# Cross-attention with LayerNorm on one core: the last 14 tiles' orders dealt anew, residual and row sum merged for eight tiles, and the last step of five tiles shared by three engines

## The chip, the core and the metric

The kernel runs on one core of a Trainium2 chip. The core has a matrix engine (TensorE, PE in the profile), three engines for elementwise work (VectorE or DVE, ScalarE or ACT, GpSimd or POOL), a queue engine (SyncE, SP), and 16 DMA engines that serve the queues. The metric is the device time of one execution in microseconds (us); smaller is better. Times given as medians come from several executions; the profile shows one execution.

## The reference

```python
qs = (q @ wq).reshape(Bq, Lq, H, HD).transpose(0, 2, 1, 3)      # q = x, 4 x 2048 rows of 512
ks_ = (k @ wk).reshape(Bq, Lk, H, HD).transpose(0, 2, 1, 3)     # k = v = context, 4 x 77 rows of 512
vs = (v @ wv).reshape(Bq, Lk, H, HD).transpose(0, 2, 1, 3)
scores = jnp.einsum('bhqd,bhkd->bhqk', qs, ks_) / jnp.sqrt(jnp.float32(HD))
scores = jnp.where(mask[:, None, :, :], -jnp.inf, scores)
attn_w = jax.nn.softmax(scores, axis=-1)
attn = jnp.einsum('bhqk,bhkd->bhqd', attn_w, vs).transpose(0, 2, 1, 3).reshape(Bq, Lq, H * HD)
out = attn @ wo + q
mu = jnp.mean(out, axis=-1, keepdims=True)
var = jnp.mean((out - mu) ** 2, axis=-1, keepdims=True)
return (out - mu) / jnp.sqrt(var + EPS) * gamma + beta
```

16 heads of 32, float32 throughout, 8192 rows of x, a padding mask over the 77 keys.

## The kernel before

The 8192 rows are 64 tiles of 128 rows. Four tiles make a group (queries are projected for a group at a time), two tiles a block (attention is applied to a block at a time). float32 products are made of three passes over high and low parts, so a projection of 128 x 512 is 12 matmuls.

The order of all work is written out by hand: `ORDER` is one long string of words, and each word issues a few instructions. Each engine runs its own instructions in the order of the string and waits, where it must, for data, for a buffer or for one of the eight PSUM banks, which `SLOTS["mm"]` deals out one by one. So a word's place in the string matters only against words of the same engine and queue. A word is a letter with a tile, block or visit number:

| word | engine | what it does (line) |
|---|---|---|
| `Q`, `q` | PE, DVE | project queries (L292), copy them out of PSUM (L306) |
| `S` | PE | scores of a tile, 64 narrow matmuls (L429) |
| `T`, `e` | DVE, ACT | row maxima of four heads (L446), their exponentials with row sums (L461) |
| `r`/`h`, `n`/`m`, `t` | DVE, POOL, DVE | reciprocal sums (L471, L482 by halves), weights times them (L476, L488 by halves), transpose (L497) |
| `P`, `U` | SP, POOL or ACT queue (last letter `s`, `g`, `a`) | one of twelve transfers that regroup a block's or a tile's weights (L508) |
| `V`, `W` | PE | weights times values for a block (L522) or a tile (L537), narrow matmuls |
| `a`/`c`, `b`/`d` | ACT, DVE | high part (L551) and low part (L555) of that product, out of PSUM |
| `O` | PE | output projection of a tile, 12 matmuls (L603) |
| `!`, `^` | PE, ACT | open a bank with one matmul (L577), seed it with x (L580), so that `O` adds to x |
| `+`, `$` | DVE | residual to SBUF (L606) or left in PSUM (L609) |
| `s`, `=` | DVE, ACT | mean and variance by bn_stats (L650, L652), or by a Copy pass and a Square pass with sums (L656, L657) |
| `u`, `@` | POOL | one over the root (L663 to L666), or that and a shift (L670) |
| `y`, `z`, `>` | DVE | centre and times gamma (L679); times the root, plus beta (L682), by halves (L686) |
| `%`, `k` | ACT | scale and shift (L674, L635) |
| <code>&#124;</code>, `f` | POOL | times gamma or plus beta (L642), one pass or both |
| `w`, `<`, `x`, `g` | SP (half a `<` on ACT) | store of a tile (L645) or half (L692), loads |
| `i`, `j`, `v`, `M` | ACT, POOL, POOL, DVE | split x for the next group, root for two earlier tiles, mask |

Up to tile 47 all tiles are finished the same way: `+ s v k f w`. From tile 48 on (`LATE`) each tile has its own mix of the words above. `o_proj` from tile 50 on puts the four matmuls that need the low part last. Before the change, PE's order from S50 to the end is

```
S50 V22 S51 Q54 Q55 O45 O44 S52 V23 S53 Q56 Q58 S54 O46 Q59 S55 Q57 V24 O47 S56 O48 V25 S57 O49 O51
S58 Q61 Q62 Q63 S59 Q60 V26 S60 O50 V27 S61 O53 O52 S62 O54 S63 O55 V28 V29 O57 !63 O56 !58 O59 V30
O58 O61 O60 W62 W63 O62 O63
```

and ACT's order behind its last exponential is `^58 ^63 %50 =56 a30.1 a30.0 =55 U63.0a %54 U63.1a =58 =59 =61 c62 %57 =60 c63 =62 =63 <63.1`.

## Time and profile before

| | |
|---|---|
| median of 3 runs | 506.64 us (506.02 to 507.09) |
| the profiled execution | 507.38 us, span 505.5 us |
| TensorE clock granted | 0.996 |
| busy share | PE 98%, DVE 93%, ACT 94%, POOL 82% |
| share of the last chain on PE | 96% |
| bytes moved | 110.97 MB, 220 GB/s |

The span is the time from the first instruction to the last; the execution's own time is longer by 1.9 us around it. Times in the views are counted from the start of the span. A row of the groups reads: line, engine, operation, output <- input, shapes, count | busy us, mean ns of one | idle time of the engine just ahead of them and what ended it. A row of the timeline reads: start, length, engine, line, operation; a row of the chain: start, length, engine, tile and line.

### The profile page before, as it was taken

To read this page: it belongs to the slowest core of one execution; us is meant where nothing else is said; L and a number is where in the kernel's file an instruction comes from. 1 tells how busy PE (TensorE), PEld (TensorE's weight loads), DVE (VectorE), ACT (ScalarE), POOL (GpSimd) and SP (SyncE) were. 2 spreads that over 40 slices of the span, in tenths; PEclk is the share of its full clock that TensorE was granted. 3 is DMA by queue.
4 is the path that set the end of the run, shared out by engine and by line. 5 is a ranking of instruction groups with operands and counts; after the bars stand their busy time and mean duration, and the time that the engine had idled before them with its cause. 6 is when DMAs were issued, how large, how long until landed. Compare 5 with 4: busy or idle time off the path is not lost.

```text
span 505.5 us, 21829 instructions
## 1 busy us (share of the span) xinstructions
PE 496.0 (98%) x6834; PEld 383.8 (76%) x6834; DVE 468.4 (93%) x2556; ACT 473.1 (94%) x2252; POOL 414.5 (82%) x380
## 2 busy tenths in 40 slices
PE   9999999999999999999999999999999999999994
PEld 7987777777777777777778777777877777777772
DVE  5798999999999999999999999999999999999996
ACT  6698999998999999999999999999999999999973
POOL 3664756989978998988899898889989869888894
PEclk9999999999999999999999999999999999999998
DMA  8947768868987676696777687787778787678656
GB/s 302 398 146 219 190 181 193 251 171 241 250 228 234 201 228 192 207 258 201 223 215 232 196 241 202 222 226 219 212 203 231 208 226 234 180 208 223 161 167 260
DMA packets 59521, 110.97 MB, mean 220 GB/s; under 512 B 9441, under 2 KB 12283, under 8 KB 59410
## 3 DMA queue, kind: packets, MB, share of 16 engines
q1 hardware_dynamic: 56658, 103.99, 70.9%
q0 software_dynamic: 2224, 5.05, 3.5%
q8 instruction: 60, 0.98, 0.9%
q10 hardware_dynamic: 528, 0.52, 0.3%
q14 instruction: 51, 0.42, 0.3%
HBM read 41.79 MB, written 16.78 MB: 116 GB/s over the span
## 4 chain that ended last, share of the span: by engine, by line
PE 96%; POOL 1%; DMA 1%; ACT 1%; DVE 0%; issue 0%; DVEq 0%
PE pq L292 35%; PE po L603 34%; PE pa L522 11%; PE sc L429 11%; PE pq L746 1%; PE pk L315 1%; PE pv L354 1%; DMA first_xtl<-xw 1%; POOL xth L642 1%; PE pv L342 0%; POOL mvt L666 0%; ACT AH L551 0%; PE pa L537 0%; DVE xtl L682 0%; ACT xth L674 0%
## 5 line engine op out<-in xcount | busy, mean ns | idle before, releaser
L461 ACT ACTIVATE pbuf<-pbuf,nm 128x77 f32<-128x77 f32 x1024 | 352.6, 351 | 3.7 <-DVE nm L446 3.7
L461 ACT ACTIVATION_READ_ACCUMULATOR pbuf<-pbuf,nm 128x1 f32 x1024 | 196.4, 192 | 0.0
L446 DVE CUSTOM_DVE_ANT_0 pbuf<-sc,mb 128x77 f32<-128x77 f32 x1024 | 171.2, 234 | 6.9 <-PE sc L429 3.7
L476 POOL TENSOR_TENSOR pbuf<-pbuf,ri 128x1232 f32<-128x1232 f32 x63 | 142.7, 2266 | 30.5 <-DVE ri L471 29.1
L603 PE MATMUL po<-woh,AH 128*128 128x512 f32 x256 | 101.6, 397 | 0.0
L292 PE MATMUL pq<-xth,wqh 128*128 128x512 f32 (+1 forms) x256 | 101.4, 396 | 0.2
L603 PE MATMUL po<-wol,AH 128*128 128x512 f32 x256 | 99.9, 390 | 0.0
L292 PE MATMUL pq<-xtl,wqh 128*128 128x512 f32 (+1 forms) x256 | 98.4, 384 | 0.0
L292 PE MATMUL pq<-xth,wql 128*128 128x512 f32 (+1 forms) x256 | 98.2, 383 | 0.0
L497 DVE STREAM_TRANSPOSE B<-pbuf 128x1280 f32<-128x1280 f32 x64 | 96.2, 1503 | 1.6 <-POOL pbuf L476 0.5
L603 PE MATMUL po<-woh,AL 128*128 128x512 f32 x256 | 93.0, 390 | 0.0
L446 DVE DVE_READ_ACCUMULATOR2_ANT nm<- 128x1 f32 x1024 | 85.6, 84 | 0.0
L275 POOL TENSOR_TENSOR xtl<-xtf,xth 128x1024 fp32r<-128x1024 f32 x28 | 67.2, 2403 | 4.3 <-ACT xth L271 4.3
L642 POOL TENSOR_TENSOR o<-o,bet 128x512 f32<-128x512 f32 x51 | 65.9, 1292 | 3.8
L429 PEld LDWEIGHTS sc<-kct,q 32*64 32x64 f32 x4096 | 51.5, 130 | 22.3 <-issue 11.5
L642 POOL TENSOR_TENSOR o<-o,gam 128x512 f32<-128x512 f32 x51 | 67.0, 1313 | 0.0
L429 PE MATMUL sc<-kct,q 32*64 32x77 f32 x4096 | 60.9, 238 | 0.0
L522 PE MATMUL pa<-PT,vsb 96*32 96x256 f32 x992 | 59.5, 382 | 0.0
L603 PEld LDWEIGHTS po<-woh,AH 128*128 128x128 f32 x256 | 48.0, 188 | 12.7 <-issue 1.2
L292 PEld LDWEIGHTS pq<-xth,wqh 128*128 128x128 f32 x256 | 48.1, 188 | 12.5 <-issue 1.2
L603 PEld LDWEIGHTS po<-woh,AL 128*128 128x128 f32 x256 | 47.9, 188 | 10.6 <-DVE AL L555 0.6
L292 PEld LDWEIGHTS pq<-xth,wql 128*128 128x128 f32 x256 | 48.1, 188 | 9.8
(135 smaller groups left out, 638.5 us busy)
## 6 DMA issues: line engine op xcount, KB each, us to landing
PT<-B SPq DMA_DIRECT2D x351, 128.0 KB
xtf<-xT SPq DMA_DIRECT2D x28, 512.0 KB
o<-x SPq DMA_DIRECT2D x56, 256.0 KB
out<-o SPq DMA_DIRECT2D x56, 256.0 KB
PT<-B POOLq DMA_DIRECT2D x20, 128.0 KB, 4.0
PT<-B SPq DMA_DIRECT2D x17, 64.0 KB
stage_a<-wk SPq DMA_DIRECT2D x4, 256.0 KB
stage_a<-xT SPq DMA_DIRECT2D x2, 512.0 KB
```

The lines of the kernel that those rows point to most:

```text
L275: nc.gpsimd.tensor_tensor(l[:, c : c + 2], fx.pop((g, c)), xh[g][:, c : c + 2].bitcast(F32), ALU.subtract)
L292: nc.tensor.matmul(pq, w[:, c, m * P : (m + 1) * P], r[g][:, c, rs], start=(n == 0), stop=(n == 11))
L315: nc.tensor.matmul(pks[m][:, : NB * NK], w[:, c, m * P : (m + 1) * P], ctx_s[c][i], start=(c == 0 and n == 0), stop=(c == NC_D - 1 and n = ...
L354: nc.tensor.matmul(pv[: rows.stop - rows.start], ctx_s[c][i][:, rows], v[c], start=(n == 0), stop=(n == 11))
L429: mm = nc.tensor.matmul(sc[j][r0 : r0 + SR, g * NK : (g + 1) * NK], qs[q, g, rs.start + r0 : rs.start + r0 + SR], kct[q, g, t // TPB, keys ...
L446: nc.vector.tensor_tensor_reduce(pb[:, h // 2, (h % 2) * NK : (h % 2 + 1) * NK], scs[t][j][:, g * NK : (g + 1) * NK], mb[:, t % TPB, keys_ ...
L461: nc.scalar.activation(pb[:, h // 2, (h % 2) * NK : (h % 2 + 1) * NK], pb[:, h // 2, (h % 2) * NK : (h % 2 + 1) * NK], AF.Exp, bias=nmax[t ...
L476: nc.gpsimd.tensor_tensor(pv, pv, rv.to_broadcast((P, NP, 2, NK)), ALU.mult)
L497: nc.vector.transpose(bt.rearrange("p c q r -> p q c r"), pbuf[t % NPB].rearrange("p q (c r) -> p q c r", c=5),)
L522: nc.tensor.matmul(pas[b, g // 2][HD * j : HD * (j + 1), (g % 2) * BLK : (g % 2 + 1) * BLK], vsb[:, 2 * b // TPB, h % 2, HD * (h // 2) : H ...
L603: nc.tensor.matmul(pos[t], a[:, c, rs], w[:, c, :], start=(first and i == 0), stop=(i == len(terms) - 1))
L642: nc.gpsimd.tensor_tensor(od[t], od[t], (gam, bet)[i], (ALU.mult, ALU.add)[i])
```

## The change

`ORDER` is rewritten from the words around S50 to the end, on all engines and queues, with PSUM banks dealt anew for it; everything ahead stays. New words:

- `{` (`residual_sum`): one VectorE instruction adds the residual in PSUM and gives the row sum; a second, of one column, makes the negative mean. `}` (`squares`): ScalarE's Square pass for the variance. Tiles 48, 52, 53, 56, 57, 58, 60 and 63 take this pair in place of `$ s` or `$ =`.
- `-` (`root_act`): ScalarE's Sqrt on one column, `?` (`inverse`): VectorE's reciprocal of it. Tiles 50, 52, 53, 56, 58, 59, 61, 62 and 63 take these in place of GpSimd's `u`; `;` is the shift of tile 50 on VectorE.
- `_` (`scale_centred`): for tiles 51, 57, 58, 59 and 60 VectorE centres into SBUF (`y`), ScalarE multiplies by the root (`_`), GpSimd adds beta (`|`) where VectorE's `z` did both.

One bank is opened with a matmul (`!62`) instead of two (`!58`, `!63`). The profile before has one ACT_TABLE_LOAD, at the start; the first Sqrt (`-50`) stands behind the last exponential. Tile 63 is now projected ahead of tile 62. Transfers for regrouping: SP 83 (before 89), GpSimd 34 (25), ScalarE 0 (3). The new orders:

```
PE from S50: S50 V22 S51 Q55 Q54 Q57 S52 V23 S53 Q59 O44 O45 S54 Q56 Q58 S55 V24 S56 O47 Q63 Q60 O46
  S57 V25 S58 O49 O48 Q61 S59 Q62 V26 S60 O51 O50 S61 V27 O52 S62 O53 S63 O54 V28 O55 O57 V29 O56 O58
  V30 O59 O60 O61 !62 W63 W62 O63 O62
ACT behind the last exponential: a29.1 }57 %55 -50 }56 }53 a30.1 -53 a30.0 }58 -56 _51 }52 -58 %49 =54
  _57 =59 _58 -52 %50 c63 ^62 c62 -59 }60 =61 _59 -61 }63 _60 -63 =62 -62 <63.1
DVE behind t63: {58 ?50 y53 b30.1 y56 ;50 b30.0 ?53 ?56 $59 y58 ?58 z56 y54 y52 z53 z54 $61 {60 ?52 y59
  d63 z52 ?59 d62 y60 {63 y61 ?61 z61 y63 ?63 >63.0 >63.1 y62 ?62 z62
POOL behind the last `n`: u51 P30.5g U62.6g @55 m63.1 m63.0 |55.0 u57 U63.6g U63.8g U63.9g U63.7g U63.3g
  |51.1 |49.0 u54 |55.1 |57.1 |49.1 |58.1 |50.0 u60 |50.1 |59.1 |60.1
```

The code of the diff, with the last lines of the string:

```diff
@@ -114,32 +114,32 @@
...
-y55 @57 U63.9s z56 O60 U63.4s =59 $61 |54.0 U63.10s y58 w53 z52 =61 u59 z55 |50.1 W62 $60 W63 y59 c62 |54.1 w50 y61
-%57 w56 d62 O62 =60 u58 w54 z59 w46 w55 u61 z58 c63 |57.0 z61 $62 w61 w58 d63 O63 |57.1 =62 w52 y60 u60 w57 y62 w59
-u62 =63 z60 z62 w60 u63 y63 w62 >63.1 >63.0 <63.1 <63.0
...
+y58 =54 |49.0 U62.8s ?58 z56 w51 O61 _57 y54 u54 =59 y52 |55.1 z53 z54 _58 w53 !62 |57.1 W63 $61 -52 %50 {60 W62 |49.1
+w57 c63 w56 ?52 y59 ^62 c62 d63 O63 |58.1 w49 -59 w47 z52 }60 ?59 d62 =61 |50.0 w58 w54 y60 w52 O62 w55 {63 _59 u60
+y61 -61 |50.1 }63 ?61 z61 _60 |59.1 y63 w50 -63 =62 w61 ?63 >63.0 >63.1 |60.1 w59 <63.0 -62 y62 <63.1 ?62 z62 w60 w62
...
+    on_act = {int(word[1:]) for word in ORDER.split() if word[0] == "_"}
...
         nc.scalar.activation(od[t], pos[t], AF.Square, bias=mv[:, 3:4], accum_out=mv[:, 1:2])
+        means[t] = mv[:, 3:4]
         by_act.add(t)
+
+    def residual_sum(t):
+        mv = mvs[t, 1] = tiny.tile([P, 4], F32, tag="mvt", bufs=64 - LATE, name=f"mvt_{t}")
+        mn = tiny.tile([P, 2], F32, tag="mnt", bufs=1, name=f"mnt_{t}") if t == 63 else mv[:, 2:4]
+        means[t] = mn[:, 1:2]
+        nc.vector.tensor_tensor_reduce(pos[t], pos[t], od[t], 1.0, 0.0, ALU.add, ALU.add, accum_out=mn[:, 0:1])
+        nc.vector.tensor_scalar(means[t], mn[:, 0:1], -1.0 / D, None, ALU.mult)
+        by_act.add(t)
+
+    def squares(t):
+        mv = mvs[t, 1]
+        nc.scalar.activation(od[t], pos[t], AF.Square, bias=means[t], accum_out=mv[:, 1:2])
...
+    def root_act(t):
         mv = mvs[t, 1]
-        nc.gpsimd.tensor_scalar(mv[:, 3:4], mv[:, 0:1], mv[:, 2:3], -1.0, ALU.mult, ALU.mult)
+        nc.scalar.activation(
+            mv[:, 2:3], mv[:, 1:2], AF.Sqrt, bias=eps[:, :1], scale=1.0 / D if t in by_act else 1.0
+        )
+
+    def inverse(t):
+        nc.vector.reciprocal(mvs[t, 1][:, 2:3], mvs[t, 1][:, 2:3])
+
+    def shift_one(t, eng=nc.gpsimd):
+        mv = mvs[t, 1]
+        if t in by_act:
+            eng.tensor_scalar(mv[:, 3:4], means[t], mv[:, 2:3], None, ALU.mult)
+        else:
+            eng.tensor_scalar(mv[:, 3:4], mv[:, 0:1], mv[:, 2:3], -1.0, ALU.mult, ALU.mult)
...
     def centre(t):
         o = pos.get(t, od[t])
-        m, op = (3, ALU.add) if t in by_act else (0, ALU.subtract)
-        nc.vector.scalar_tensor_tensor(o, o, mvs[t, 1][:, m : m + 1], gam, op, ALU.mult)
+        if t in on_act:
+            pos.pop(t, None)
+            to = od[t]
+        elif t == 63:
+            to = pos[t] = bank(f"pc_{t}")
+        else:
+            to = o
+        m, op = (means[t], ALU.add) if t in by_act else (mvs[t, 1][:, 0:1], ALU.subtract)
+        nc.vector.scalar_tensor_tensor(to, o, m, gam, op, ALU.mult)
+
+    def scale_centred(t):
+        nc.scalar.activation(od[t], od[t], AF.Copy, scale=mvs[t, 1][:, 2:3])
```

More of the change, by code (lines that the diff above doesn't have):

```diff
@@ L116 @@
 P22.8s f38 k41 P22.5s T49.0 a21.1 Q53 g29 e48.2 T49.2 x47 r47 b21.1 n47 e48.3 b21.0 T49.3 T49.1 O43 e48.0 M52.4 f41
-q53 e49.0 t47 O42 e49.3 q52 P23.7s r48 w38 +43 i28 n48 P23.2s s43 k40 P23.4s S50 +42 e49.2 w41 V22 j28 T50.1 P23.10s
-T50.0 P23.6s e50.1 T50.2 P23.1s S51 s42 x46 a22.0 P23.0s e49.1 T50.3 Q54 v21 P23.3s t48 P23.9s f40 k43 P23.11s T51.0
-P23.8s a22.1 Q55 e50.2 T51.2 P23.5s r49 g30 b22.1 x49 n49 e50.3 b22.0 T51.3 T51.1 O45 e50.0 q55 f43 t49 e51.0 q54
-P24.7s O44 e51.3 r50 w40 +45 n50 P24.4s s45 e51.2 P24.3s P24.9s S52 i29 +44 x63 P24.2g M60.4 P24.11s V23 e51.1 T52.2
@@ L121 @@
-P24.1g P24.5s j29 T52.0 P24.6s e52.2 T52.3 S53 P24.0s t50 x51 e52.3 Q56 P24.8s r51 T52.1 n51 a23.0 T53.0 e52.1 s44 Q58
-q56 a23.1 v22 e52.0 T53.2 b23.0 b23.1 P24.10a t51 S54 k44 e53.0 O46 r52 P25.3g P25.7s T54.1 n52 g31 T53.3 e53.2 P25.6s
-T53.1 w43 T54.0 e53.1 Q59 P25.2s T54.3 f44 x60 T54.2 e53.3 P25.11s t52 P25.5s e54.0 P25.9s S55 M56.4 P25.1s r53 +46
-Q57 n53 e54.1 q59 P25.10s T55.0 P25.0s e54.3 T55.2 P25.8s q58 P25.4g V24 e54.2 q57 t53 a24.0 x56 O47 T55.3 P26.6s
-a24.1 r54 x59 s46 e55.2 n54 x48 P26.1s T55.1 P26.8s k42 b24.1 w44 S56 b24.0 P26.9s k45 f42 t54 P26.11s i31 O48 P26.10s
@@ L126 @@
-e55.3 T56.1 T56.0 x52 j31 x57 e55.0 T56.3 P26.4s V25 $48 w42 P26.2s +47 i30 P26.3s T56.2 P26.0g S57 a25.0 P26.7s s48
-j30 e55.1 O49 b25.0 T57.0 a25.1 T57.1 e56.1 r55 T57.3 n55 b25.1 O51 e56.3 T57.2 $49 e56.0 P26.5g t55 S58 e57.0 s49
-P27.1g P27.7s Q61 P27.4g P27.5s s47 e56.2 u49 P27.9s T58.1 P27.11s u48 y48 e57.3 P27.3g T58.0 v23 Q62 +51 e57.1 y49
-r56 z49 n56 e57.2 T58.2 w49 Q63 x58 q61 P27.6s e58.1 z48 P27.8s P27.2g q62 w48 f45 e58.0 x53 T58.3 x50 P27.0s t56 S59
-P27.10s e58.3 Q60 r57 q63 n57 w45 e58.2 T59.2 T59.3 k46 T59.0 V26 e59.3 q60 f46 t57 e59.0 S60 r58 P28.7s T59.1 n58 O50
@@ L131 @@
-e59.2 P28.10s s51 x54 T60.1 P28.11s a26.0 P28.2s T60.0 a26.1 P28.3s P28.5g T60.3 e59.1 P28.8g P28.4s V27 T60.2 P28.6s
-b26.1 k47 P28.1s r59 b26.0 n59 e60.0 P28.0s S61 t58 P28.9s O53 a27.0 +50 a27.1 t59 e60.2 e60.1 T61.0 P29.1g P29.3s O52
-b27.1 P29.2g P29.0s P29.7g T61.3 P29.4s e60.3 P29.11g T61.1 P29.8s P29.10g T61.2 P29.5s e61.3 @51 S62 P29.9s r60 $52
-x62 b27.0 n60 O54 P29.6s e61.0 T62.0 T62.2 e61.2 T62.3 f47 T62.1 S63 e61.1 t60 O55 %51 r61 T63.1 n61 w47 e62.2 x55 +54
-T63.2 e62.1 T63.3 V28 |51.0 t61 e62.3 V29 |51.1 T63.0 P30.8s a28.0 s52 P30.5s a28.1 P30.10g P30.1s $53 e62.0 P30.6g
@@ L136 @@
-P30.11s b28.1 P30.7g P30.2s b28.0 O57 u52 a29.1 P30.9s r62 s50 a29.0 n62 P30.4s e63.0 s53 P30.0s !63 O56 P30.3s b29.0
-e63.1 b29.1 u53 +57 @50 e63.3 t62 !58 O59 e63.2 y53 U62.11s U62.10g U62.4g U62.7s z53 U62.2g ^58 U62.5s h63.0 h63.1
-$56 m63.1 ^63 U62.1s y52 V30 %50 U62.6s s54 m63.0 =56 U62.8s x61 $55 U62.9s U62.0g O58 t63 a30.1 w51 u56 U62.3s a30.0
-=55 @54 b30.0 U63.11s b30.1 U63.6s U63.3g U63.0a s57 O61 U63.5s |50.0 %54 U63.2s $59 U63.1a U63.7s y56 u55 =58 U63.8s
-y55 @57 U63.9s z56 O60 U63.4s =59 $61 |54.0 U63.10s y58 w53 z52 =61 u59 z55 |50.1 W62 $60 W63 y59 c62 |54.1 w50 y61
@@ L141 @@
-%57 w56 d62 O62 =60 u58 w54 z59 w46 w55 u61 z58 c63 |57.0 z61 $62 w61 w58 d63 O63 |57.1 =62 w52 y60 u60 w57 y62 w59
-u62 =63 z60 z62 w60 u63 y63 w62 >63.1 >63.0 <63.1 <63.0
+q53 e49.0 t47 O42 e49.3 q52 P23.7s r48 w38 +43 i28 n48 P23.2s s43 k40 P23.4s P23.8s M60.4 P23.11s e49.2 w41 P23.6s +42
+S50 P23.9g V22 j28 T50.0 T50.2 e49.1 P23.5s T50.3 P23.10s S51 t48 i29 x49 P23.3g P23.1s Q55 P23.0g a22.1 T50.1 e50.2
+b22.1 r49 T51.2 n49 e50.1 T51.3 Q54 T51.1 a22.0 e50.0 j29 t49 Q57 e50.3 q54 P24.6s T51.0 P24.7g g31 e51.2 M56.4 P24.1s
@@ new lines @@
+P24.0g q55 P24.8s P24.10g b22.0 e51.0 S52 P24.9s r50 q57 n50 g30 V23 T52.3 P24.11s e51.1 T52.0 P24.3s T52.1 f40 e51.3
+S53 t50 P24.4s Q59 a23.1 r51 x46 T53.1 e52.1 T53.3 P24.2g T53.2 P24.5g e52.3 s42 n51 O44 T52.2 a23.0 e53.1 b23.1 b23.0
+v21 e52.2 O45 +44 T53.0 e52.0 t51 e53.2 S54 s44 P25.2s P25.4g P25.3s +45 Q56 P25.6g e53.0 P25.5s r52 q59 n52 P25.9s
+T54.1 e53.3 P25.8s T54.0 w40 T54.3 x60 Q58 i30 P25.0g T54.2 r53 t52 e54.2 n53 q56 e54.3 S55 x57 q58 j30 V24 T55.2 x51
+k43 T55.1 i31 T55.0 S56 t53 e54.0 P25.1g P25.7g O47 j31 a24.0 T56.3 P26.3s e54.1 T56.1 P25.11s T56.2 P25.10s e55.1
@@ new lines @@
+T56.0 P26.0s Q63 f43 T55.3 P26.11s a24.1 s45 x62 e55.3 b24.0 r54 +47 Q60 w43 n54 e56.1 P26.7s s47 P26.9s q63 e55.2
+P26.10s P26.5g P26.1s t54 O46 v22 e55.0 x48 P26.6s q60 x56 e56.2 b24.1 P26.4g x61 P26.2s r55 P26.8g n55 S57 +46 k44
+e56.3 V25 T57.3 T57.2 k42 T57.0 f44 S58 T57.1 e56.0 s46 O49 e57.1 t55 v23 w44 x59 a25.1 r56 P27.0s T58.3 k45 P27.1g
+O48 P27.8s T58.0 a25.0 n56 P27.3s b25.1 e57.2 P27.7s +49 b25.0 P27.9s e57.0 T58.1 x63 Q61 f42 P27.5s s49 e57.3 P27.10s
+T58.2 x50 t56 P27.2s e58.3 x58 P27.11g S59 P27.4s {48 e58.2 w42 Q62 r57 T59.0 n57 q61 k46 T59.1 }48 T59.2 e58.1 f46
@@ new lines @@
+V26 q62 T59.3 x52 e58.0 t57 S60 a26.0 u48 y48 O51 P28.2s e59.3 P27.6g b26.0 w46 P28.7s P28.5g z48 a26.1 @49 P28.10s
+r58 e59.0 b26.1 P28.4s T60.1 O50 n58 P28.9s T60.3 e59.1 w48 T60.2 P28.11s T60.0 P28.6s e59.2 P28.8g t58 P28.3s S61
+P28.0s e60.2 V27 P28.1s +50 x53 r59 T61.0 e60.1 n59 T61.2 O52 T61.3 a27.0 T61.1 e60.0 f45 b27.0 t59 e60.3 S62 P29.10s
+a27.1 r60 O53 T62.3 P29.3g e61.1 P29.7s n60 T62.2 x54 b27.1 P29.6s e61.2 T62.0 P29.4s T62.1 P29.0s S63 P29.9g e61.0
+t60 w45 P29.8g O54 P29.1s P29.2g e61.3 P29.11s T63.3 P29.5s T63.0 e62.1 r61 T63.2 n61 x55 V28 T63.1 k47 $51 e62.3 $54
@@ new lines @@
+f47 O55 t61 a28.1 a28.0 b28.1 P30.2s e62.2 s51 P30.9s P30.3g P30.11s b28.0 O57 e62.0 P30.4g {52 P30.10s P30.1s e63.1
+r62 y51 n62 P30.6s s50 P30.0s V29 e63.3 P30.8s $55 P30.7s u51 t62 e63.2 O56 P30.5g s55 a29.0 U62.2s e63.0 U62.6g
+U62.3s b29.0 @55 U62.5s {57 a29.1 U62.0s h63.1 h63.0 }57 m63.1 {56 U62.7s %55 b29.1 O58 U62.1s m63.0 -50 y57 U62.9s
+{53 U62.10s V30 |55.0 U62.4s }56 t63 U62.11s }53 u57 O59 a30.1 {58 U63.11s -53 U63.6g a30.0 U63.0s ?50 y53 U63.8g }58
+U63.2s U63.9g b30.1 -56 _51 U63.10s U63.7g y56 U63.3g U63.4s }52 ;50 b30.0 O60 |51.1 U63.1s -58 ?53 ?56 $59 %49 U63.5s
@@ L149 @@
         "5071263450231746052371462750136427051320465731206457261340752631402357160423751627405361270453201647"
-        "3520614726531074263510234756012374562710436527014320561734206517264350712654032057104627510423576013"
-        "2745032417230547621347065430712634107531043710573105252364"
+        "3520614726531074263510234756012374562710436527014320561734205176451062734651456072435106274301513046"
+        "25137052462734105723401567304256307470263672076172606271430"
     ),
@@ L260, in xattn_layernorm @@
     od, pos, mvs, rns, vd, ris, parts = {}, {}, {}, {}, {}, {}, {}
-    ends, tmps, xs, by_act = {}, {}, {}, set()
+    ends, tmps, xs, by_act, means = {}, {}, {}, set(), {}
+    on_act = {int(word[1:]) for word in ORDER.split() if word[0] == "_"}
     pe_words = [w for w in ORDER.split() if w[0] in "HBQSVWXO"]
@@ L666, in rsqrt_one @@
         nc.gpsimd.tensor_tensor(mv[:, 2:3], mv[:, 2:3], mhalf[:, :1], ALU.pow)
-    def shift_one(t):
+    def root_act(t):
         mv = mvs[t, 1]
-        nc.gpsimd.tensor_scalar(mv[:, 3:4], mv[:, 0:1], mv[:, 2:3], -1.0, ALU.mult, ALU.mult)
+        nc.scalar.activation(
[9 more added lines that the diff above has]
+            eng.tensor_scalar(mv[:, 3:4], mv[:, 0:1], mv[:, 2:3], -1.0, ALU.mult, ALU.mult)
     def scale_one(t):
@@ L795, in xattn_layernorm @@
         "!": lambda k, part: open_bank(k), "^": lambda k, part: seed(k),
+        "-": lambda k, part: root_act(k), "?": lambda k, part: inverse(k),
+        ";": lambda k, part: shift_one(k, nc.vector),
+        "{": lambda k, part: residual_sum(k), "}": lambda k, part: squares(k),
+        "_": lambda k, part: scale_centred(k),
         "@": lambda k, part: (rsqrt_one(k), shift_one(k)), "%": lambda k, part: scale_one(k),
```

## The prediction

> **What bounds the kernel now.** The page comes first: who is busy, and what the chain that ended last is made of.

> ```profile
> span 505.5 us, 21829 instructions
> PE 496.0 (98%) x6834; PEld 383.8 (76%) x6834; DVE 468.4 (93%) x2556; ACT 473.1 (94%) x2252; POOL 414.5 (82%) x380
> PE 96%; POOL 1%; DMA 1%; ACT 1%; DVE 0%; issue 0%; DVEq 0%
> ```

> PE carries 96% of the chain. Stage by stage, with the columns PE, PEld, DVE, ACT, POOL, clock:

> ```profile
> 460.00:476.00 16.00, 16.00 (x177) 11.56 (x176) 15.55 (x83) 15.78 (x82) 15.59 (x17) 1.00 0.74 201
> 476.00:490.00 14.00, 14.00 (x98) 10.26 (x100) 13.30 (x23) 11.60 (x32) 11.89 (x23) 1.00 0.59 163
> 490.00:505.50 15.50, 7.38 (x80) 5.54 (x72) 10.60 (x17) 6.06 (x15) 9.14 (x15) 0.87 0.64 240
> ```

> PE, DVE and ACT are full until 476, POOL nearly; one that falls behind stops PE. From 490 nobody is full: latency bounds the end. The chain in order of time (start, length) prices PE's work; the last rows here are the chain's end:

> ```profile
> 380.02 0.93 PE sc L429 x54
> 380.95 1.86 PE pa L522 x32
> 382.81 0.88 PE sc L429 x56
> 383.69 5.66 PE pq L292 x24
> 389.36 5.44 PE po L603 x24
> 476.17 0.23 PE po L577
> 489.61 1.05 PE pa L537 x32
> 498.61 0.56 POOL mvt L666
> 499.19 0.75 DVE xtl L682
> 499.94 0.68 DVE po L679
> ```

> The timeline at the end:

> ```profile
> 491.17 1.08 PE L537 MATMUL pa<-PT,vsb 96*32 96x128 f32 x32 [0.55 <-DVE po L609]
> 496.84 1.09 PE L603 MATMUL po<-woh,AL 128*128 128x512 f32 x4
> 497.97 0.60 ACT L656 ACTIVATE xtl<-po 128x512 f32<-128x512 f32 x1 [0.34 <-PE po L603]
> 498.69 0.69 ACT L657 ACTIVATE xtl<-po,mvt 128x512 f32<-128x512 f32 x1
> 499.27 0.19 ACT L657 ACTIVATION_READ_ACCUMULATOR xtl<-po,mvt 128x1 f32 x1
> 499.83 0.55 POOL L666 TENSOR_TENSOR mvt<-mvt,small 128x1 f32<-128x1 f32 x1
> 500.71 0.88 DVE L686 SCALAR_TENSOR_TENSOR xtl<-po,mvt,bet 128x256 f32<-128x256 f32 x2
> 501.97 0.33 SPq L692 DMA_DIRECT2D out<-xtl  x1
> ```

> The last matmul ends at 497.93. Statistics, POOL's root and VectorE's halves take until 501.59; the last store is issued at 501.97, and 3.53 us later the span ends.

> **The change part by part.**

> PE's stream. S50 starts at 380.02, and ahead of it PE's order is unchanged. A score visit costs 0.88, a product V 1.86, a W 1.05, an O or Q 2.72 (5.44/2), and the first full-array visit after narrow ones 5.66 - 5.44 = 0.22 more (0.25 taken, since single visits later take 2.92 to 3.00). Before: 14 x 0.88 + 9 x 1.86 + 2 x 1.05 + 30 x 2.72 + 16 switches x 0.25 + 2 opened banks x 0.23 = 117.2, so 497.2; the remainder to 497.93 is the pipe's 0.2 and the 0.5 that W63 waits. After: 14 switches and one opened bank, 116.5. **Gain 0.7.**

> W63's wait. The profile names VectorE, but W63 reads tile 63's regrouped weights, whose transfers are issued behind its transpose. What each engine does there:

> ```profile
> 476.85 0.58 ACT L580 COPY po<-xth 128x512 f32<-128x512 f32 x1
> 479.16 2.54 POOL L488 TENSOR_TENSOR pbuf<-pbuf,ri 128x616 f32<-128x616 f32 x2
> 481.73 1.51 DVE L497 STREAM_TRANSPOSE B<-pbuf 128x1280 f32<-128x1280 f32 x1 [0.53 <-POOL pbuf L488]
> 482.67 6.43 SPq L508 DMA_DIRECT2D PT<-B  x10
> 481.05 1.08 ACT L551 CAST AH<-pa 128x512 fp32r<-128x512 f32 x2 [0.36 <-PE pa L522]
> L674 ACT ACTIVATE o<-o,mvt 128x512 f32<-128x512 f32 x3 | 2.4, 813 | 0.8 <-POOL mvt L670 0.8
> L657 ACT ACTIVATE xtl<-po,mvt 128x512 f32<-128x512 f32 x4 | 2.8, 688 | 0.1
> L461 ACT ACTIVATE pbuf<-pbuf,nm 128x77 f32<-128x77 f32 x1024 | 352.6, 351 | 3.7 <-DVE nm L446 3.7
> L740 ACT ACT_TABLE_LOAD x1 | 1.3, 1283 | 1.2 <-PEq L848 1.2
> ```

> ACT's exponentials end at 476.85. Ahead of that the change takes one scaling (0.81), one transfer issue (0.6) and one cast (0.5) off ACT and adds one Square (0.68): end at 475.6. Then reciprocals, POOL's 2.54 and the transpose: it ends at 480.1 where it ended at 483.2. SP issues seven of tile 63's twelve transfers, not ten in 6.43: 4.5 us, and one of tile 62's. So the weights are there by 488, PE reaches W63 at 488.7, and the 0.5 goes. **Gain 0.5**, if nothing else is late.

> What is late next is ACT. Behind its last exponential it now has five Squares, two two-pass statistics, three casts, three scalings, three scalings of centred tiles, five roots and a load of another function table ahead of c63, which O63 needs. One instruction overlaps its predecessor by 0.07 (two casts of 572 ns take 1.08), so: 5 x 0.68 + 2 x 1.39 + 3 x 0.52 + 3 x 0.74 + 3 x 0.63 + 5 x 0.22 + 1.28 = 14.2, and 475.6 + 14.2 = 489.8. (A centred scaling lies between the 688 ns with one per-row operand and the 813 with two; a root of one column is 351 - 76 x 0.775 = 292 ns, the slope from 77 to 512 columns.) W63 ends at 489.8 and PE spends until 491.1 on W62 and the switch; c63 needs 0.58. Slack 0.7: **0**. The load's only row is the start's. Its bounds: hidden in ACT's waits (0), or paid twice, 2.57; I take one, as the row has it.

> [...]

> VectorE, GpSimd, queues.

> ```profile
> L606 DVE TENSOR_TENSOR o<-po,o 128x512 f32<-128x512 f32 x51 | 33.9, 665 | 9.8 <-PE po L603 9.8
> L446 DVE CUSTOM_DVE_ANT_0 pbuf<-sc,mb 128x77 f32<-128x77 f32 x1024 | 171.2, 234 | 6.9 <-PE sc L429 3.7
> L642 POOL TENSOR_TENSOR o<-o,gam 128x512 f32<-128x512 f32 x51 | 67.0, 1313 | 0.0
> L508 POOL DMA_DIRECT2D PT<-B x25 | 14.1, 566 | 7.7 <-DVE ri L471 2.9 <-DVE B L497 2.2 <-PE sc L429 1.6
> L650 DVE BATCH_NORM_STATS2 st<-po 128x6 f32<-128x512 f32 x4 | 2.7, 681 | 0.0
> L482 DVE RECIPROCAL ri<-sum 128x8 f32<-128x8 f32 x2 | 0.3, 172 | 0.0
> ```

> The merged residual and sum has no row: below, a plain residual's 0.67 plus 0.1 for the mean; above, 512 columns at 234/77 ns each, 1.56. It is one pass over 512 columns like the residual, so 0.8. After S50 VectorE loses seven residuals, four bn_stats and three finishing passes and gains eight merged passes and, net, six small ones: -4.7 - 2.7 - 2.25 + 6.4 + 1.0 = -2.2. ACT loses four two-pass statistics, a scaling, a seeding copy and three transfer issues and gains eight Squares, nine roots, five centred scalings and the load: about +3. POOL loses seven roots (0.85 with the sum ahead) and two root-and-shift pairs (1.1) and gains three passes (1.31) and nine issues (0.57): about +1. SP issues 83 regroupings instead of 89.

> VectorE's cover: behind t63 (480.1) its list sums to 13.0 until tile 63's merged pass, so it is there at 493.1, while O63 ends at 494.0; at 1.56 a piece the two merged passes on the way make it 0.6 late, and with its own the end by 1 or so, which stays inside the range. New waits on it are the reciprocals, each behind a root of ACT: the one of tile 52 (root at 489.1) holds tile 59's centring and d63, which O63's last four matmuls need at 492.9 and which by the same sum ends at 492.1.

> POOL has no cover. From 478.5 it has eleven passes, three roots and five issues: 14.4 + 2.7 + 2.9 = 20.0, back to back until 498.5, when tile 60's store can go; SP holds tile 62's store behind that one. Five of the passes wait for a centred scaling on ACT, by the sum above each at hand 0.5 us or more before POOL gets there; that of tile 49 waits for a plain scaling that comes just in time.

> Between 380 and 476 I take 0: by sums of the same durations, each bank or weight that a PE visit needs is free 0.3 us (S53, S63, V28) or more ahead. The margin is thin, hence a rival; the other end is 1.5, one late product.

> The end. PE drains at 496.7. Copy and Square as before, 1.55: 498.3; root 0.3, reciprocal and two hand-overs 0.35: 499.0; finish 0.75: 499.75; store issued at 499.95. Last issue to end 3.53, plus 0.3 because 256 KB go where 128 went:

> ```profile
> GB/s 177 410 118 0 41 0 261 353 15 108 394 405 404 405 405 410 405 405 410 410 410 405 405 410 179 404 210 384 272 0 212 156 279 33 15 0 0 0 0 0
> ```

> (128 KB at 405 GB/s.) End 503.8, against 505.5: -1.7, of which 0.7 and 0.5 above and 0.5 in the tail, where a root on ACT replaces POOL's 0.55 and VectorE no longer waits behind POOL (498.61, 499.19, 499.94 in the chain). Four chains meet within 0.5 us there (c63 and W62; tile 60's store and tile 62's; VectorE's centring and the root; O63 and its merged sum); hand-overs at such meetings cost 0.31 and 0.34 in the rows above, one is sure to count: +0.4. **Sum -1.3.** The profiled execution took 507.38 in all, 0.74 above the median 506.64; by the median: 505.3.

> **Rivals.**

> *Late ACT, slower.* In order, c63 stands behind everything above. If the exponentials end 1 us later than before instead of 1.2 earlier (ACT is full to 476, so any wait for a score shifts all), and the load counts twice, c63 starts at 489.8 + 2.2 + 1.3 = 493.3, O63 at 493.9 instead of 491.1: -1.3 + 2.8 = +1.5, 508.1. It decides from a lateness of 3.0 at c63. For it: ACT's 15.78 of 16 before 476. Against: that work is less than before.

> *The tail doesn't shorten.* PE's 0.7 comes, but POOL's 20.0 us stretch by 2.2 where a pass waits for ACT's scaling; tile 62's store then goes behind tile 60's at 501.2 and the span ends at 505.0: 506.1, no change. For it: POOL has no slack left. Against: it was idle for long before 476 and can be early.

> *The load holds ACT for twice its row.* At 2 x 1.28 c63 comes 1.3 later and O63 0.7: 506.0, no change. For it: ACT has no slack between its last exponential and c63 but those 0.7. [...]

> *PE stalls in the middle.* One product (V24 and V28 come 2.7 earlier in PE's stream, by one visit) that waits 1.5 for weights: 506.8, no change.

> **How the numbers follow.** About 0.2%, 1.0 us, is what can be told from no change. Chances: forecast (1.0 to 2.2 less, 504.4 to 505.6) 0.50, since PE's lighter stream and the earlier transpose rest on counts; tail 0.14; the doubled load 0.10; middle 0.08; late ACT, or a longer stall, 0.18, since it needs 3 us. So faster 0.50, same 0.32, slower 0.18. To leave out 2 in 10 the range goes from 504.3 (no meeting charged, 504.9, less half of the 1.07 by which the runs spread) to 507.9, just short of late ACT.

> **What would show it.** Right: PE's last matmul ends near 496.7, 1.2 earlier; W63 without a wait; one further table load, 1.28, followed directly by a root; the last transpose at 480; the last store issued by 500.3. Wrong: a PE gap ahead of O63 named after ACT's cast (late ACT, or the load); more than one further load; SP waiting for POOL's last pass with tile 62 finished (the tail); a gap ahead of V24, V28 or S63; the merged pass above 1.2 us.

## The result, and the profile after

| | median, us | lowest to highest | runs |
|---|---|---|---|
| before | 506.86 | 506.02 to 507.22 | 6 |
| after | 509.92 | 509.07 to 510.63 | 6 |

The ratio is 1.0063, with a 95% interval from 1.0052 to 1.0074: the change made the kernel slower, by 3.1 us, where 1.3 less was forecast. The profiled execution after the change took 509.07, its lowest, against a span of 507.2.

The page of the kernel after it, in the same parts as before:

```profile
span 507.2 us, 21832 instructions
...
PE 496.1 (98%) x6833; PEld 384.4 (76%) x6833; DVE 466.6 (92%) x2572; ACT 477.6 (94%) x2265; POOL 416.4 (82%) x372
...
q8 instruction: 60, 0.98, 0.9%
...
PE 98%; issue 1%; DVE 0%; ACT 0%
```

VectorE, ScalarE and GpSimd are about as busy as before. What is new is the word "issue" with 1% in the chain that ended last: time in which the engine waited for nothing that the profile shows. The chain in order of time (start, length) has it in one place, and is otherwise TensorE's work from end to end:

```profile
378.78 0.88 PE sc L430 x53
...
391.28 0.90 PE sc L430 x50
392.17 1.86 PE pa L523 x32
394.04 0.42 PE sc L430 x22
394.46 3.48 issue
397.93 1.11 PE sc L430 x42
399.04 3.90 PE pq L293 x12
402.94 5.44 PE po L604 x24
...
493.17 1.88 PE pa L538 x64
495.05 5.68 PE po L604 x24
```

The kernel before has the same three visits, S52, V23 and S53, without a stop:

```profile
394.80 0.88 PE sc L429 x57
395.68 1.86 PE pa L522 x32
397.54 0.88 PE sc L429 x55
```

After the change S53's scores stop after 22 of 64 matmuls, and TensorE stands for 3.48 us. The other 42 then take 1.11 instead of 0.46, and the projection behind them (Q59) 3.90 instead of the 2.92 of a first one behind narrow work. The view by stretches, with PE's busy time first and clock, DMA share and GB/s last, says why the work after the gap is slow:

```profile
388.00:390.00 2.00, 2.00 (x10) 1.39 (x9) 2.00 (x9) 2.00 (x13) 2.00 (x2) 1.00 0.01 4
...
394.00:396.00 2.00, 0.46 (x26) 0.30 (x22) 1.83 (x6) 2.00 (x12) 1.92 (x3) 1.00 1.09 234
396.00:398.00 2.00, 0.07 (x8) 0.07 (x10) 0.00 (x0) 2.00 (x13) 1.98 (x4) 0.91 0.99 261
398.00:400.00 2.00, 2.00 (x45) 1.65 (x46) 0.95 (x11) 1.12 (x6) 2.00 (x1) 0.50 1.05 220
```

The granted clock is 0.50 behind the gap. The trace's clock record has half speed for 3.41 us from 397.62 on. So the place costs 3.48 + 0.65 + 0.98 = 5.1 us. Without it this execution would be at about 504.0 and, if all six lost as much, the median at 504.8, close to the 505.3 of the forecast. The same rows show the DMA engines idle from 388 to 390 and full from 394 on. Everything else of the change has to be looked for with the gap out of the way, so the first question was what TensorE waits for in the middle of a visit whose queries, keys and banks were all in use already.

A lead is the row of queue q8 on the page, which the page of before has word for word: 60 packets, 0.98 MB, 16 KB each, of the kind "instruction". TensorE's records (matmuls, weight loads, NOPs, semaphore instructions) number 15,417, one packet for every 257, and in the trace the packets, each of 16,384 bytes, start between 16.86 and 494.36 us. So q8 is read here as TensorE's code, which comes through the DMA engines while it runs, in blocks of about 257 instructions, taken as 256 (the table of fetches below has what speaks for it). (From here on a block without a number is such a block of code, its edge is the place where the next one begins, and a fetch is the packet that brings one; block 24 and the like are still pairs of tiles.) The block of code that TensorE was working off when it stopped, the block in hand, was entered at 389.94. In the view of the DMA engines from there to 395.2, the queues are

```profile
q1 hardware_dynamic: 315, 0.82, 66.2%
q0 software_dynamic: 120, 0.34, 22.2%
...
xtf<-xT SPq DMA_DIRECT2D x2, 512.0 KB
...
PT<-B POOLq DMA_DIRECT2D x3, 128.0 KB, 7.6
```

with no packet of q8, and in the next 1.4 us (395.2 to 396.6) stands the missing one:

```profile
q8 instruction: 1, 0.02, 6.0%
```

By the trace's records it starts at 395.24 and lands at 396.58; TensorE's next instruction is at 397.93.

### The profile page after: what moved, and what is told of

Read it like the earlier page. It is cut to its first block, busy times and chain, and to the rows that moved or that the text cites. A ratio compares the mean times of both kernels' runs of the same rounds, so it can differ in the third digit from the quotient of the medians.

```text
span 507.2 us, 21832 instructions
## 1 busy us (share of the span) xinstructions
PE 496.1 (98%) x6833; PEld 384.4 (76%) x6833; DVE 466.6 (92%) x2572; ACT 477.6 (94%) x2265; POOL 416.4 (82%) x372
## 4 chain that ended last, share of the span: by engine, by line
PE 98%; issue 1%; DVE 0%; ACT 0%
PE po L604 35%; PE pq L293 35%; PE pa L523 11%; PE sc L430 11%; PE pk L316 1%; PE pq L782 1%; PE pv L355 1%; PE pw L740 1%; PE pa L538 0%; PE pv L343 0%; ACT xtl L658 0%; DVE po L712 0%; DVE xtl L718 0%; ACT xtl L657 0%; PE po L578 0%
## 5 line engine op out<-in xcount | busy, mean ns | idle before, releaser
L447 DVE DVE_READ_ACCUMULATOR2_ANT nm<- 128x1 f32 x1024 | 84.2, 82 | 0.0
L643 POOL TENSOR_TENSOR o<-o,bet 128x512 f32<-128x512 f32 x52 | 67.2, 1293 | 3.8
L643 POOL TENSOR_TENSOR o<-o,gam 128x512 f32<-128x512 f32 x51 | 67.0, 1313 | 0.0
```

Source lines behind the costliest of these rows:

```text
L447: nc.vector.tensor_tensor_reduce(pb[:, h // 2, (h % 2) * NK : (h % 2 + 1) * NK], scs[t][j][:, g * NK : (g + 1) * NK], mb[:, t % TPB, keys_ ...
L643: nc.gpsimd.tensor_tensor(od[t], od[t], (gam, bet)[i], (ALU.mult, ALU.add)[i])
```

## The experiments

**Two theories.** *Late code*: TensorE ran out of instructions. By this theory a block of 256 has to be there when the one in hand is used up; the fetch is asked for on entering the block in hand, and waits behind data. (No record shows when a fetch is asked for, so this is an assumption; a fetch's wait is the time from the entry to the start of its packet.) *A late product*: S53 waits for data or a buffer that the profile does not name, which is the forecast's own rival in the middle. The first predicts that moving the blocks' edges, or the transfers, closes the gap; by the second neither does.

**Edges moved.** NOPs already stand between the projections' matmuls; one character of a string sets how many for each visit. Six more in each of ten visits ahead of S52 move every later edge by 60 instructions.

```diff
-    "...kkkkkkkjkkk00"
+    "...qqqqqqqpqqk00"     # visits 87 to 96 of 124: 20 NOPs become 26, one 19 becomes 25
```

> The changed kernel with 60 more idle instructions (NOPs) in TensorE's stream, six in each of the ten projection visits ahead of S52; order, data, buffers and transfers are the changed kernel's. Theory 1, late code: TensorE stops in S53 because the 16 KB block of instructions that it needs next has not arrived; two score visits and a V use up the block in hand in 4.52 us, while the fetch asked for on entering that block started 5.30 us later behind data. With the blocks' edges moved by 60 instructions the block in hand starts in the projections ahead of S52 (at 386.3 instead of 389.9) and lasts 7.2 us; so no gap in S53, no stretch at half clock: 5.0 us less (3.48 of gap, 0.60 and 0.96 more in the two visits at half clock), 504.9. Theory 2, a late product: S53 waits for data that the profile does not name; NOPs change nothing in that, the gap of about 3.5 stays and the time is 509.9.

Measured: 504.70 (504.24 to 505.32) against 506.67 before in the same set, 0.9962 (0.9947 to 0.9976). The chain has no gap, and no slow visit:

```profile
393.68 1.86 PE pa L523 x32
395.54 0.88 PE sc L430 x53
396.42 2.92 PE pq L293 x12
```

NOPs alone, 60 among 15,417 records, gave back 5.2 us. A late product is out: data, order and buffers are the same, and S53 runs from 395.54 to 396.42 without a stop, earlier than the 397.93 at which the changed kernel could go on.

**One load moved.**

```diff
-S52 P24.9s r50 q57 n50 g30 V23 ... O45 +44 T53.0
+S52 P24.9s r50 q57 n50 V23 ... O45 +44 g30 T53.0
```

> The changed kernel with one of the two 512 KB loads of xT, the one issued at 392.5 behind S52, issued behind O45 instead, after S53. TensorE's instructions are untouched, so the short block of 4.52 us stays. Theory 1, late code: the fetch waits behind one load instead of two, as the other fetches next to one load did (2.2 to 3.6 us); with 0.9 to 1.6 for the packet and 1.35 to the first instruction the gap in S53 is 0 to 1.9 instead of 3.48, and no half clock follows: 504.9 to 506.8. Theory 2, a late product: the load is not an input of S53's scores; the gap stays, 509.9.

Measured: 509.69 (507.94 to 510.47) against 506.67, 1.0058 (1.0035 to 1.0081). The gap stays:

```profile
395.00 3.20 issue
...
398.97 4.53 PE pq L293 x12
```

A miss for the size that theory 1 gave, since the fetch still waited 5.06 us. The load that was moved, issued 2.6 us behind the entry, hardly matters: the wait is 0.24 shorter without it. The other one is issued 0.2 ahead of the entry; it was not moved alone.

**Both loads moved.**

```diff
-P24.6s T51.0 P24.7g g31 e51.2 ... n50 g30 V23 ... O45 +44 T53.0
+P24.6s T51.0 P24.7g e51.2 ... n50 V23 ... O45 +44 g31 g30 T53.0
```

> The changed kernel with both 512 KB loads of xT (issued at 389.7 and 392.5) issued behind O45 instead, after S53. Theory 1, late code: the fetch waits 0.6 to 1.9, as those without a load beside them did, and arrives before the short block of 4.52 us is used up: no gap, 504.9, unless the later loads hold up the casts of group 14 and 15 on ScalarE. Theory 2, a late product: 509.9 with the gap.

Measured: 505.43 (504.96 to 506.63) against 506.67, 0.9981 (0.9971 to 0.9990).

```profile
394.70 1.23 issue
395.93 0.77 PE sc L430 x41
396.70 2.95 PE pq L293 x12
```

The gap is 1.23, not 0, because the fetch still waited 3.31, now beside the regrouped weights alone, as the next run bears out; no half clock follows it. Most of the loss is gone, and TensorE's code was not touched.

**All of it moved.** The twelve transfers of block 24's weights too, in the changed kernel's own code blocks.

```diff
-Q57 ... P24.6s ... P24.7g g31 ... P24.1s P24.0g ... P24.8s P24.10g ... P24.9s ... g30 ... P24.4s ... P24.5g ... O45 +44
+Q57 ... O45 +44 P24.6s P24.7g P24.1s P24.0g P24.8s P24.10g P24.9s P24.11s P24.3s P24.4s P24.2g P24.5g g31 g30
```

> The changed kernel with its own block edges, and with all that was issued between Q57 and S54 for later use issued behind O45 instead: the twelve transfers of block 24's weights and both 512 KB loads of xT. With the loads alone moved, the fetch still waited 3.31 us and the gap was 1.23. If the fetch waits for whatever data stands in the DMA engines' queues: 0.6 to 1.9 of wait, as at most other edges, and with 0.9 to 1.6 for the packet and 1.35 to 1.5 to the first instruction the short block of 4.5 us just suffices or falls short by up to 0.5: 504.4 to 505.2. If short blocks are the whole cause and the traffic is not: the gap of 1.23 stays, 505.4. Block 24's weights land some 7 us later, by about 409, ahead of V24 at 412.

Measured: 505.66 (504.83 to 507.53) against 506.52, 0.9983 (0.9971 to 0.9996). In the profiled execution the fetch waited 1.64 and the block landed just in time: no gap.

```profile
395.29 0.88 PE sc L430 x54
396.17 2.92 PE pq L293 x12
```

The trace bears theory 1 out, the median lies 0.5 above the range given. Why it stays 0.7 to 1.0 above the kernel with the moved edges is open. From S50 to the last matmul its trace (380.03 to 496.93) takes 0.07 less than that of the kernel with the moved edges (379.82 to 496.79 in its second profile), so the profiled execution shows nothing more that was lost. The fetch has no room to spare here, so some executions may still stop; no trace shows one.

**The stall made in the kernel before.** If the theory holds, it must be possible to put the gap into the old order. First try: 60 fewer NOPs and a later load.

```diff
-P23.5s r49 g30 b22.1 x49 ... f43 t49 e51.0 q54 P24.7s
+P23.5s r49 b22.1 x49 ... f43 t49 e51.0 q54 g30 P24.7s     # and kkkkkkjkkk -> eeeeeedeee
```

> The kernel before with 60 fewer NOPs in TensorE's stream ahead of S52 (six fewer in ten projection visits) and the 512 KB load of xT that was issued at 388.5 issued some 5 us later, about 1 us ahead of S52. Nothing else differs. Theory 1, late code: a block of instructions now begins at S52's first scores and is used up in 3.2 us by S52, V23 and half of S53; the fetch waits 2.2 to 3.6 behind the load, 0.9 to 1.6 for the packet and 1.35 to the first instruction follow, so a gap of 1.3 to 3.3 appears in S53 of a kernel that had none: 508.2 to 510.2. Theory 2, a late product of the new order: the order is the old one, so no gap and 506.9.

Measured: 506.51 (506.08 to 508.91) against 506.67, 1.0006 (0.9990 to 1.0021): no gap, a miss on both counts. The load was issued at 387.7, since SyncE had nothing to wait for ahead of it. And the fetch started at 390.92, 2.1 us ahead of the first instruction of the block in hand: while slow matmuls of projections are worked off, the part of TensorE that reads the instructions runs ahead of them, across the edge. The trace shows it so: the semaphore instructions of S52's scores stand at 389.6 to 390.3, their first matmul at 393.58. A short block (3.56 us) alone cost nothing here. Second try, with the edge in the middle of S52 and the load behind a transfer that waits:

```diff
-P23.5s r49 g30 b22.1 x49 ... q54 P24.7s O44
+P23.5s r49 b22.1 x49 ... q54 P24.7s g30 O44     # and kkkkkkjkkk -> 8888887888: twelve NOPs fewer each
```

> The kernel before with 120 fewer NOPs ahead of S52 (twelve fewer in ten projection visits) and the 512 KB load that was issued at 388.5 put behind the next transfer of regrouped weights, so that it is issued at about 393.5. With 60 fewer TensorE had run ahead of the block's edge while the projections were still being worked off, and the load was issued at 387.7 all the same; now the edge lies in the middle of S52, where nothing is waiting to be worked off. Theory 1, late code: the block from the middle of S52 to the end of S53 lasts 3.2 us; the fetch waits 2 to 3.5 beside the load, 0.9 to 1.5 for the packet and 1.4 to the first instruction follow: a gap of 1 to 3.2 in or right behind S53, 507.7 to 509.9. Theory 2, the stall needs the new order's data: no gap, 506.7.

Measured: 512.22 (510.33 to 515.48) against 506.65, 1.0112 (1.0071 to 1.0154). The chain of the old order now has the gap, 60 matmuls into S53:

```profile
397.65 0.85 PE sc L429 x51
398.50 2.46 issue
400.96 0.35 PE sc L429 x4
```

The gap is in the range, the median above it. The profiled execution, at 510.33, is the lowest of four. From the trace of before to this one the end of the last matmul moves from 497.93 to 500.81, by 2.9, of which the gap is 2.46. What the other three lost more isn't shown; the record has granted clocks of 0.986, 0.993 and 0.996 for them (0.997 for the profiled one), the lowest for the slowest.

**The fetch in eight kernels.** From the traces' records, in us. "Entered" is the first instruction of the block in hand, counted in steps of 256 from the place where the changed kernel stopped; a few lost records make it uncertain by some instructions.

| kernel | entered | fetch starts | lands | block in hand lasts | next block begins | gap | then at half clock |
|---|---|---|---|---|---|---|---|
| before | 390.10 | 392.30 | 393.18 | 7.4 | 397.47 | 0 | no |
| after | 389.94 | 395.24 | 396.58 | 4.5 | 397.93 | 3.48 | 3.41 |
| one load moved | 390.48 | 395.54 | 396.88 | 4.5 | 398.20 | 3.20 | 3.41 |
| both loads moved | 390.16 | 393.47 | 394.40 | 4.5 | 395.93 | 1.23 | no |
| all moved | 391.17 | 392.81 | 393.94 | 4.2 | 395.42 | 0 | no |
| edges moved | 387.52 | 389.28 | 390.15 | 7.2 | 394.72 | 0 | no |
| old order, first try | 393.04 | 390.92 | 392.25 | 3.6 | 396.61 | 0 | no |
| old order, second try | 395.09 | 398.36 | 399.64 | 3.4 | 400.96 | 2.46 | no |

The four gaps end 1.32 to 1.53 after the block lands, and in all four the first instruction behind the gap is the same one by number, the 12,737th of TensorE's records, 22 matmuls into S53 in the new order and 60 in the old. So the sum that fits all eight is: the wait, plus about 1.1 for the packet, plus 1.35, against the time that the block in hand lasts. Worked out with each landing for 46 blocks of each of the thirteen profiles, it gives a stop in four places, the four gaps. Both sides are needed. In a second profile of the kernel with the moved edges the next fetch waited 5.82 us, longer than the one that stopped the changed kernel, and cost nothing, since the block in hand lasted 10.07. The end of Q57, S52, V23 and 22 matmuls of S53 use up 256 instructions in 4.5 us; between edges 12 and 57 of the profiles of before and after no other block is shorter than 5.2, and of all fetches there in the thirteen profiles the median wait is 1.1: most fetches start soon after the block in hand is entered. Counted in steps of 256, the middle half of the waits between these edges lies within 0.97 us before and 0.85 after; in steps of 255 or 257 it takes 1.10 to 1.28.

**The parts of the change, one at a time.** With the stall gone, each of the three new mechanisms was undone on the kernel with the moved edges (504.7).

```diff
-{56 ... }56 ... {53 ... }53      # merged residual and sum, Square on ScalarE (eight tiles)
+$56 ... =56 ... $53 ... s53      # residual; Copy and Square (56, 58, 60, 63) or bn_stats (48, 52, 53, 57)
```

> The kernel with the shifted blocks (504.7), with the merged residual and sum undone for all eight tiles: a plain residual into PSUM, then Copy and Square on ScalarE for tiles 56, 58, 60 and 63, and bn_stats on VectorE for 48, 52, 53 and 57, as the kernel before did. The base's rows, from the start of one instruction to the next: merged pass with its mean 0.84, plain residual 0.59, bn_stats with its aggregate 0.82, Copy 0.71, Square 0.62. VectorE gets 8 x -0.25 + 4 x 0.82 = +1.3, ScalarE 4 x 0.71 - 4 x 0.62 = +0.4. If VectorE's sum sets the end (it is idle for 0.4 us between 480 and 496): +0.5 to +1.3, 505.2 to 506.0. If TensorE's stream hides it: no change, 504.7.

Measured: 506.57 (505.95 to 507.55) against 506.65, 0.9998 (0.9989 to 1.0008), so 1.9 more. More than expected, and for another reason: TensorE comes to W62 and W63 only 0.45 later than without the edit, but there the chain goes over to ScalarE and stays there until 500.04, the end of its last Square.

```profile
490.03 1.05 PE pa L538 x32
...
491.10 0.58 ACT AH L552
...
494.28 0.59 ACT xtl L657 x2
...
499.25 0.79 ACT xtl L658 x2
```

The Copy passes of tiles 60 and 63 stand in that queue with those of 61 and 62; its sum over the whole tail (+0.4) did not tell that all four fall into its last 9 us.

```diff
--53 ... ?53 ... -63 ... ?63      # root on ScalarE, reciprocal on VectorE (nine tiles)
+u53 ... u63                      # GpSimd's root
```

> The kernel with the shifted blocks (504.7), with the nine roots and reciprocals on ScalarE and VectorE replaced by GpSimd's root at the same places in the order; no further function table is loaded. ScalarE: -9 x 0.19 - 1.28 = -3.0. GpSimd: eight times sum and root 0.80, one root 0.55: +7.0, and it is idle for only about 1 us between 479.4 and its end at 498.7. If GpSimd's chain becomes the end: its last pass ends near 505 and the roots of tiles 63 and 62 stand in that queue, so about +6 to +7: 510.7 to 511.7. If the load and roots held ScalarE more than they relieved GpSimd: 504.7 or less.

Measured: 511.94 (511.60 to 512.33), 1.0100 (1.0085 to 1.0115): +7.2, 0.2 above the range; the chain is GpSimd's, as expected, until VectorE's last pass.

```profile
500.53 1.24 POOL o L643
...
503.34 0.55 POOL mvt L680
503.89 1.23 POOL xtl L643
```

```diff
-_59 ... |59.1      # ScalarE scales, GpSimd adds beta (51, 57, 58, 59, 60)
+z59                # VectorE does both
```

> The kernel with the shifted blocks (504.7), with the last step of tiles 51, 57, 58, 59 and 60 given back to VectorE alone: one pass that scales and adds beta in place of ScalarE's scaling and GpSimd's pass. From the base's rows, start to start: VectorE +5 x 0.66 = +3.3, ScalarE -5 x 0.61 = -3.1, GpSimd -5 x 1.25 = -6.2. VectorE is idle for 0.4 us between 480 and 496 and makes the low parts that O63 and O62 need, so if VectorE bounds there: +2 to +3, 506.7 to 507.7. If GpSimd's chain had been the bound of the tail: 504.7 or less.

Measured: 508.38 (507.94 to 509.26), 1.0037 (1.0027 to 1.0047): +3.7, 0.7 above the range. The chain is VectorE's from 472 to the end, and O63 waits for its low part.

```profile
493.93 0.60 DVE AL L556
...
495.25 0.59 DVE AL L556
...
502.60 0.75 DVE xtl L718
```

The three do not add up to a sum: each was taken from a tail in which all engines end together.

**The best version.** The edges moved, with and without the loads moved as well:

> The changed kernel with the blocks' edges shifted by 60 NOPs and with both loads moved behind O45: candidate for the best version. The shift alone already leaves no gap in TensorE's stream from S50 to the end, so by theory 1 the loads are worth nothing more: 504.7 (504.2 to 505.2). If the loads cost anything besides the fetch, less: 504.2 or under.

> The changed kernel with the 60 NOPs alone, once more and with more rounds, for a narrower interval: 504.7, 0.9947 to 0.9976 of the kernel before, was measured in three.

Measured: 504.72 (504.25 to 504.96), 0.9961 (0.9948 to 0.9973), with the loads; 504.94 (504.78 to 505.37), 0.9967 (0.9955 to 0.9980), without; before 506.52 in the same set. The two can't be told apart: with the edges moved, no gain from the loads can be seen. Both beat the kernel before by 1.6 to 1.8 us and the changed one by 5.

## Why the prediction was wrong

**The step that failed** is "Between 380 and 476 I take 0", with its other end of 1.5, "one late product". It measured 5.1. The sums behind it checked banks and weights, and these were in time. What they left out was TensorE's own code: the change brings nothing new into S52, V23 and S53, but has three projections between S51 and S52 where two projections and two output products stood. With one visit fewer ahead of S52, the edge of a block came to lie 19 instructions ahead of it instead of 62. And two 512 KB loads and nine transfers of weights are issued between 389.7 and 395.2, where the fetch starts. The page of before had the row of q8, and it was passed over as 0.9% of the DMA engines' time. A rival in the middle stood in the text, at 0.08, with data as its cause and 1.5 as its size; "a longer stall" shared 0.18 with late ScalarE. The signs given for a stall there, a gap ahead of V24, V28 or S63, missed the place.

The other steps can be read from the second profile of the kernel with the moved edges, the change without its stall. The chain from S50 and at the end:

```profile
379.82 0.95 PE sc L430 x52
...
489.22 1.89 PE pa L538 x64
491.11 5.68 PE po L604 x24
...
497.52 0.79 ACT xtl L658 x2
...
498.34 0.76 DVE po L712
...
499.19 0.75 DVE xtl L718
```

- *TensorE's stream*: forecast 380.02 to 496.7, 116.7; measured 379.82 to 496.8, 117.0; before 117.9. Right, but for 0.3. In the profile of after S50 starts 1.24 earlier than before, but 0.8 of that offset is there by 21 us already, far ahead of the change, and in this profile it is 0.2.
- *W63's wait*: W62 and W63 run as one piece of 1.89. Gone, as forecast.
- *ScalarE*: some groups of the changed kernel from 470 on (busy us, mean ns, idle before):

```profile
L552 ACT CAST AH<-pa 128x512 fp32r<-128x512 f32 x7 | 4.1, 592 | 0.4 <-PE pa L538 0.4
...
L684 ACT ACTIVATE mvt<-mvt,small 128x1 f32<-128x1 f32 x9 | 2.6, 293 | 0.0
...
L666 DVE CUSTOM_DVE_ANT_0 po<-po,xth 128x512 f32<-128x512 f32 x3 | 2.0, 677 | 0.0
...
L684 ACT ACT_TABLE_LOAD x1 | 1.3, 1283 | 0.0
```

  One load, once, 1.28, a root right behind it, and no idle time ahead of it (0.0 in its row): no run shows the second 1.28 of the rival that doubled the load. ScalarE waits 0.4 for the product that c63 casts, so it was early, and neither it nor the load was the bound. A root takes 293 ns, forecast 292.
- *Merged pass*: 677 to 694 ns, 0.84 to the next instruction with its mean; forecast 0.8 and 0.15 for the mean. Right.
- *Transpose of tile 63*: forecast to end at 480.1, measured 480.9. It cost nothing, since W63 had no wait.
- *GpSimd's chain*: forecast 20.0 from 478.5 to 498.5; measured 19.3 from 479.4 to 498.7 in the first profile with the moved edges. Right.
- *The tail*: from the last matmul to the end of the span forecast 7.1, measured 6.4, before 7.6. The last store was issued at 499.97, where 499.95 was forecast; from there to the end it took 3.3, where 3.83 was taken, and the 0.4 charged for meetings didn't come. (Of the two hand-overs that priced it, 0.31 stands in the profile of before, at VectorE's centring at 497.66, and not in the rows that the prediction shows.)

Together -1.6 (504.94 against 506.52, 95% from -1.0 to -2.3), where -1.3 was the sum. The mechanisms that were argued held within a microsecond; the one that wasn't argued at all decided. That the medians came within 0.3 of the sum has some luck in it: between the two traces the span fell by 2.3 (505.5 to 503.2), since the tail was 1.1 shorter than forecast with the meetings and the stream only 0.3 longer.

## What to carry to other kernels

Where an engine's stream has thousands of small instructions (15,417 here), read its row among the instruction queues first: packets, size, and instructions for each packet. Then look for the stretch in which the engine uses up a block fastest, and ask what transfers are issued as it enters that block. A reordering moves both without any data being late; here 60 NOPs set it right (5.2 us), and two 512 KB loads issued some microseconds later gave back most of it (4.5). A wait named "issue" in the middle of a group of equal instructions was the sign of it in four profiles (3.48, 3.20, 2.46 and 1.23 us).
